# VectorE forms both halves of dt x B for the unit next to each activation table switch

## The chip, the cores and the metric

The kernel runs on one core of a Trainium2 chip. The metric is the device time of one launch in microseconds (us). The time before is the median of three runs.

## The reference

The input is a batch of 8 images of 192 channels with 56 x 56 positions, fp32. It goes through a stack of four layers: an involution (a 5 x 5 filter made from the input itself) and three selective-scan ("Mamba") layers. The scan is what matters here. For every position t of an image, every inner channel d and every one of 16 states n, each of the three layers computes

```
dt  = softplus(dbl[..., :rank] @ dt_proj.T + bias)      # dbl = xc @ x_proj.T
h   = exp(dt * A) * h + (dt * xc) * B                   # per d and n, over t
y   = sum over n of h * C   + xc * D
out = (y * silu(z)) @ out_proj.T                        # z and xc from in_proj; xc = silu(conv(...))
```

The first scan layer splits the 192 channels into three slices of 64 that share weights, each with 512 inner channels, and wraps them in layer norms. The second and third have 384 inner channels.

## The kernel before

**Tiling.** Each image is cut into 7 chunks of T = 448 positions, so there are 56 chunks. A job is one chunk of one scan: layer 1 has three jobs per chunk (168, one for each slice; i = 0, 1, 2 names the slice), layers 2 and 3 have one (56 each). The inner channels form nd groups of 128 (index j; nd = 4 in layer 1, 3 in layers 2 and 3), and the 16 states form four quarters (index q). A unit is one (job, j, q): its tile `uhg` has 128 partitions, which are 32 channels by 4 states, and 4 rows (NR) of T + 1 columns, so it covers 128 channels by 4 states. A job has nd x 4 units: 16 in layer 1, 12 in the others.

**The work of one unit k.** The rows of `uhg` are treated in two halves, h = 0 (rows 0 and 1) and h = 1 (rows 2 and 3).

- `inputs_begin` (L729, ScalarE) puts the carried state into column 0.
- `inputs_lo` (L738, VectorE) writes (dt x) B into half 0. The factor dt x is in the replica tile `reps[...][0]` in SBUF; the factor B comes from a PSUM bank, `brow`, which `spread_b` (L715, PE) fills with one matmul. The pool of this bank has one buffer, so the matmul for the next unit has to wait until the product has read the bank.
- `inputs_hi` (L734, GpSimd, called POOL below) writes (dt x) B into half 1, from `reps[...][1]` and from a copy of the same B row in SBUF, `rows[0, q]`, which a DMA brought.
- `decays` (L721, ScalarE) writes exp(dt A) into a PSUM tile for each half.
- `scan` (L742, VectorE) does the recurrence in place, one instruction for each half.
- `keep` (L746, ScalarE) copies the last column out as the carried state.
- `readout` (L751, POOL) multiplies the states by C in place, one instruction for each half.
- `reduce` (L757, L760, PE) adds the states up into `y`, and `gated` (L776, VectorE) applies silu(z).

The replica tiles are loaded by DMAs on SyncE's queue (L706, `load_ops`, two buffers) from the products dt and dt x of the job, which are stored to HBM. There are nine buffers for `uhg`.

**The loop.** `ssm_layer` issues the whole layer from one loop over the units. Each engine runs its instructions in the order of issue, and the code writes that order out by hand (`tc.manual_schedule()`), so there is no planner between the source and the queues. In iteration k come, in this order: reduction of unit k - 3, scan of half 0 of k, decays of half 0 of k + 1, `inputs_begin(k + 3)`, `inputs_hi(k + 2)`, readouts of k - 2, `inputs_lo(k + 1)`, `spread_b(k + 2)`, scan of half 1 of k, `keep(k)`, decays of half 1 of k + 1. Each iteration has two places (before the first scan, and before the second) where steps of the neighbouring jobs are run from a plan: the projections of the job to come, and the output projection of the job that has just ended (matmuls L1032 and L1034 in layer 1; L1107 in layers 2 and 3, with the addition L1113 on VectorE). `bounds` gives the places at which the stretches of the plan begin, and `places` spreads the steps over them.

**The table switches.** ScalarE's exponential and its silu and softplus need different activation tables. Once per job, a first block loads the silu table, does two activations (L587 for the coming job's xc, L568 for the running job's gate) and loads the table of the exponential again (L560). A second block does the same for the softplus (L634). `bounds` puts the first block at place `at[1]`, which is 6 in layer 1 (10 if the coming job is a slice 0) and 8 in the other layers, and the second at `at[3]`, 8 places later in layer 1 and 6 in the others. A place p belongs to iteration p // 2 of the job, so the product of that iteration on VectorE is that of unit p // 2 + 1 of the job. While a block runs, ScalarE makes no decays. Behind the first block come the matmul L592 with its copy L596 on ScalarE; behind the second come the products dt x (L641, VectorE), which read a matmul's result (L638).

**Filler.** `nothing` (L766, PE) issues matmuls with a zero weight into `y`; they do no computation.

Of the kernel before, what the change touches and what calls it, by code (L numbers as in the profile page):

```python
# [81 lines left out]
def conv_mamba_stack(ctx: ExitStack, tc: tile.TileContext, a, out):  # L82
    nc = tc.nc
# [478 lines left out]
    def with_gates(ops, u):  # L562


        def all_ops():
            ops()
            if u is not None:
                nc.scalar.activation(u.zs, u.zs, AF.Silu)  # L568

        table_block(all_ops)  # L570
# [113 lines left out]
    def ssm_layer(pool, w, jobs, n_slots):  # L684
# [10 lines left out]
        reps, brow, uhg, ys = {}, {}, {}, {}  # L695
# [15 lines left out]
        def spread_b(k):  # L711

            i, j, q = units[k]
            brow[k] = banks.b.tile([128, 512], F32, tag="b", name="b")
            nc.tensor.matmul(brow[k][:, :T], lhsT=pick_b[:, q, :], rhs=us[i].parts, start=True, stop=True)  # L715

        def decays(k, h):
            i, j, q = units[k]
            t = banks.da[h]
            for r in range(2):  # L720
                nc.scalar.activation(  # L721
                    t[:, 64 + 449 * r : 512 + 449 * r], reps[k // NQ][h][:, r, 0, :], AF.Exp, scale=w.neg_a[:, j * NR + 2 * h + r, q : q + 1]
                )

        def inputs_begin(k):
            i, j, q = units[k]
            uhg[k] = pool.tile([128, NR, T + 1], F32, tag="uhg", name="uhg", bufs=9)
            before = zeros[:, :NR] if jobs[i][1] else carry[jobs[i][0]][:, j, q, :]
            nc.scalar.copy(uhg[k][:, :, 0:1], before.unsqueeze(2))  # L729

        def inputs_hi(k):
            i, j, q = units[k]
            b = us[i].rows[0, q].unsqueeze(1).to_broadcast([128, 2, T])
            nc.gpsimd.tensor_mul(uhg[k][:, 2:4, 1:], reps[k // NQ][1][:, :, 1, :], b)  # L734

        def inputs_lo(k):
            b = brow[k][:, :T].unsqueeze(1).to_broadcast([128, 2, T])
            nc.vector.tensor_mul(uhg[k][:, 0:2, 1:], reps[k // NQ][0][:, :, 1, :], b)  # L738

        def scan(k, h):  # L740
            v = uhg[k][:, 2 * h : 2 * h + 2, :].rearrange("p r t -> p (r t)")
            nc.vector.tensor_tensor_scan(v, banks.da[h][:, 63:961], v, 0.0, ALU.mult, ALU.add)  # L742

        def keep(k):
            i, j, q = units[k]
            nc.scalar.copy(carry[jobs[i][0]][:, j, q, :].unsqueeze(2), uhg[k][:, :, T:])  # L746

        def readout(k, h):
            i, j, q = units[k]
            v = uhg[k][:, 2 * h : 2 * h + 2, 1:]  # L750
            nc.gpsimd.tensor_mul(v, v, us[i].rows[1, q].unsqueeze(1).to_broadcast([128, 2, T]))  # L751

        def reduce(k):
            i, j, q = units[k]
            if q == 0:
                ys[k // NQ] = banks.y.tile([128, 512], F32, tag="y", name="y")
                nc.tensor.matmul(ys[k // NQ][:, :T], lhsT=w.dd[:, j, :], rhs=us[i].xc[:, j, :], start=True, stop=False)  # L757
            y = ys[k // NQ]
            for r in range(NR):
                nc.tensor.matmul(y[32 * r : 32 * r + 32, :T], lhsT=fold, rhs=uhg[k][:, r, 1:], start=False, stop=(q == NQ - 1))  # L760

        def nothing(k, n):

            if k >= 0 and units[k][2] < NQ - 1:
                for _ in range(n):
                    nc.tensor.matmul(  # L766
                        ys[k // NQ][:, : nd * 112], lhsT=zeros, rhs=w.dd.rearrange("p j e -> p (j e)")[:, : nd * 112],
                        start=False, stop=False,
                    )

        def load_of(steps):
            return sum(st.cost for st in steps if st.matmuls)

        def gated(g):
            i, j = groups[g]
            nc.vector.tensor_mul(us[i].zs[:, j, :], us[i].zs[:, j, :], ys[g][:, :T])  # L776

        n_places = 2 * per_job
        def bounds(job):

            silu = 8 if nd == 3 else 10 if job[0] == 0 else 6
            softplus = silu + (6 if nd == 3 else 8)
            return 0, silu, silu + 2, softplus, softplus + 1, softplus + 4, n_places

        def places(*stretches):

            plan = [[] for _ in range(n_places)]
            for steps, first, end in stretches:  # L790
                todo, debt = list(steps), 0.0
                for p in range(first, end):
                    room, closed = (sum(st.cost for st in todo) + debt) / (end - p) - debt, False
                    while todo and (room > 1e-6 and not closed or p == end - 1):
                        if (todo[0].block if p % 2 else todo[0].settles) and p < end - 1:
                            break
                        plan[p].append(todo[0])
                        closed = todo[0].closes
                        room -= todo.pop(0).cost
                    debt = max(0.0, -room)  # L800
            return plan
# [11 lines left out]
        for k in range(3):  # L813
            inputs_begin(k)
        inputs_lo(0)
        spread_b(1)
        inputs_hi(0)
        inputs_hi(1)
        decays(0, 0)
        decays(0, 1)  # L820
# [3 lines left out]
        def load_when_free(k):  # L824

            g = len(reps)
            if g < len(groups) and k >= NQ * g - NQ - 1 and groups[g][1] in us[groups[g][0]].ops:
                load_ops(g)

        for k, (i, j, q) in enumerate(units):  # L830
            m = k % per_job
            if m == 0:

                fetch, outs, rest = tail
                if i + 1 < len(jobs):
                    u = us[i + 1]
                    at = bounds(jobs[i + 1])
                    plan = places(*zip((*jobs[i + 1][2](u, us[i], outs), rest + jobs[i + 1][3](u)), at, at[1:]))
                else:
                    gates = Step(None, lambda: with_gates(lambda: None, us[i]), 0, 0.3, block=True)  # L840
                    plan = places(([gates], 4, 6), (outs + rest, 8, n_places))
                plan[3][:0] = [Step(None, fetch, 2, 0.0)]

            if i + 1 < len(jobs) and m >= per_job - NQ:
                us[i + 1].row_in(0, m - (per_job - NQ))
            if i and m < NQ:
                us[i].row_in(1, m)
            if k >= NQ + 3 and q == 3:
                gated(k // NQ - 1)
            if k >= 3:  # L850
                reduce(k - 3)

            more = 3 - math.ceil(load_of(plan[2 * m] + plan[2 * m + 1]))
            nothing(k - 3, more > 2)
            bg.run(plan[2 * m])
            nothing(k - 3, more > 0)
            load_when_free(k)
            scan(k, 0)
            if k + 1 < n_units:
                decays(k + 1, 0)  # L860
            if k + 3 < n_units:
                inputs_begin(k + 3)
            if k + 2 < n_units:
                inputs_hi(k + 2)
            if k >= 2:
                readout(k - 2, 0)
                readout(k - 2, 1)
            if k + 1 < n_units:
                inputs_lo(k + 1)
            if k + 2 < n_units:  # L870
                spread_b(k + 2)
            bg.run(plan[2 * m + 1])
            nothing(k - 3, more > 1)
            load_when_free(k)
            scan(k, 1)
            keep(k)
            if k + 1 < n_units:
                decays(k + 1, 1)
            if m == per_job - 1:
                tail = jobs[i][4](us[i])  # L880
# [249 lines left out]
    for layer, w in enumerate((w1, w2, w3), 1):  # L1130
        with ExitStack() as stack:
            scan_banks(stack)
            pool = stack.enter_context(tc.tile_pool(name=f"ssm{layer}", bufs=1))
            load_weights(pool, w)
            with tc.manual_schedule():
                if layer == 1:
                    ssm_layer(pool, w, mamba_jobs(pool, w), 3)
                else:
                    ssm_layer(pool, w, dense_jobs(pool, w, layer), 1)
# [69 lines left out]
```

## Time and profile before

| What | Value |
|---|---|
| Median of three runs | 26491.58 us (26490.21 to 26491.7) |
| The profiled execution | 26518.46 us, its span 26516.6 us, mean PE clock 0.835 |
| PE, busy | 22170.8 us, 84% |
| VectorE (DVE), busy | 22849.2 us, 86% |
| ScalarE (ACT), busy | 17021.6 us, 64% |
| GpSimd (POOL), busy | 24242.3 us, 91% |
| Layer 1's scan | from 1658 to 18108 us |
| Layer 2's scan | from 18210 to 22363 us |
| Layer 3's scan | from 22434 to 26507 us |

The profile is of one execution on the chip. Its page gives busy times by engine, and groups of instructions, one for each line, engine and shape: a group has its count, its busy time, the mean duration of one in nanoseconds, and the idle time of the engine ahead of these instructions with what ended most of it. A line of the list of waits reads: who waited, for whom, the sum in us, the number of times, and the longest. In the timeline, each line is a start in us, a duration, the engine, the line, the operation with its operands, and, in brackets, idle time before it. An engine's busy share is not by itself a bound: an engine that is nearly always busy can still be one that nobody waits for. PEld is the load of weights on PE, which overlaps matmuls. The clock column is the granted PE clock as a share of full speed.

### The profile page before, as it was taken

How to read it: one execution, taken by the hardware profiler on the slowest of the kernel's cores; microseconds unless marked ns; L12 is line 12 of the kernel's file. 1: busy time of each engine (PE TensorE's matmuls, PEld its weight loads, DVE VectorE, ACT ScalarE, POOL GpSimd, SP SyncE). 2: the span in 40 equal slices, each digit the busy share in tenths (PEclk: the TensorE clock that was granted, in tenths of full speed). 3: DMA queues.
4: the chain of work that ended last, by engine and by line, in shares of the span. 5: the costliest groups of instructions: out<-in, count | busy, mean ns of one | idle time of the engine just before them, and what ended most of it. 6: DMA issues, size and time to landing. Idle time of an engine off the chain costs nothing. (4 is left out here: it accounts for less than half of the span.)

```text
span 26516.6 us, 248987 instructions
## 1 busy us (share of the span) xinstructions
PE 22170.8 (84%) x74628; PEld 7074.0 (27%) x74628; DVE 22849.2 (86%) x17677; ACT 17021.6 (64%) x32354; POOL 24242.3 (91%) x12820
## 2 busy tenths in 40 slices
PE   9988888888888888888878888888888888888888
PEld 3322222222222222222222222222333332333332
DVE  8878888888888888888888888887888887888888
ACT  1146666666666666666666666665666666777776
POOL 4469999999999999999999999998999998999999
PEclk9987878887778787787778877878888888888888
DMA  4433333333333333333333333333344443444443
GB/s 107 110 103 121 119 118 121 119 120 120 119 118 120 120 119 118 120 121 120 117 121 118 121 116 122 119 119 107 131 134 133 134 134 120 134 134 136 140 136 123
DMA packets 1249495, 3236.48 MB, mean 122 GB/s; under 512 B 170924, under 2 KB 510916, under 8 KB 1248008
## 3 DMA queue, kind: packets, MB, share of 16 engines
q1 hardware_dynamic: 1245336, 3219.49, 37.1%
q8 instruction: 585, 9.58, 0.1%
q14 instruction: 774, 6.34, 0.1%
q10 hardware_dynamic: 2800, 1.06, 0.0%
HBM read 2502.68 MB, written 555.55 MB: 115 GB/s over the span
## 5 line engine op out<-in xcount | busy, mean ns | idle before, releaser
L742 DVE TENSOR_TENSOR_SCAN uhg<-da,uhg 128x898 f32<-128x898 f32 x8064 | 16063.3, 2013 | 1003.2 <-ACT da L721 991.9
L751 POOL TENSOR_TENSOR uhg<-uhg,rows 128x896 f32<-128x896 f32 x8064 | 15387.2, 1930 | 809.0 <-ACT carry L746 769.7
L721 ACT ACTIVATE da<-rep,k 128x448 f32<-128x448 f32 x16128 | 10262.0, 636 | 1843.9 <-DVE uhg L742 1531.9
L734 POOL TENSOR_TENSOR uhg<-rep,rows 128x896 f32<-128x896 f32 x4032 | 8407.6, 2085 | 592.2 <-DMA rep<-ops 554.0
L738 DVE TENSOR_TENSOR uhg<-rep,b 128x896 f32<-128x896 f32 x4032 | 4296.4, 1066 | 923.9 <-PE b L715 873.4
L760 PE MATMUL y<-uhg,k 128*32 128x448 f32 x32256 | 4946.3, 658 | 124.0 <-POOL uhg L751 120.6
L746 ACT COPY carry<-uhg 128x4 f32<-128x4 f32 x4032 | 787.6, 195 | 4268.1 <-DVE uhg L742 4259.3
L715 PE MATMUL b<-k,k 96*128 96x448 bf16 x4032 | 1603.6, 398 | 1903.1 <-DVE uhg L738 1895.9
L766 PE MATMUL y<-w_d,k 128*128 128x448 f32 (+1 forms) x5908 | 3015.2, 608 | 0.0
L757 PE MATMUL y<-xc,w_d 128*128 128x448 f32 x2016 | 1411.4, 793 | 835.8 <-DVE zs L776 833.5
L1008 PE MATMUL mm<-xs,k 128*128 128x448 f32 x2688 | 1345.1, 628 | 571.4 <-ACT da L721 413.1
L766 PEld LDWEIGHTS y<-w_d,k 128*128 128x128 f32 x5908 | 1174.3, 220 | 1867.8 <-issue 1841.5
L626 PE MATMUL mm<-dbl,w_dt 36*128 36x448 f32 (+1 forms) x2016 | 1580.7, 897 | 36.1 <-ACT k L608 35.5
L760 PEld LDWEIGHTS y<-uhg,k 128*32 128x32 f32 x32256 | 749.9, 116 | 3182.6 <-issue 1554.8
L1060 PE MATMUL mm<-v,w_in 96*128 96x448 f32 x2688 | 1416.4, 658 | 152.0 <-ACT zs L668 97.7
L431 POOL TENSOR_TENSOR x<-x,one 96x448 f32<-96x448 f32 x560 | 633.2, 1135 | 648.8 <-DVE one L423 631.3
L641 DVE TENSOR_TENSOR dt<-dt,mm 128x448 f32<-128x448 f32 x1008 | 609.1, 618 | 644.5 <-PE mm L638 469.5
L715 PEld LDWEIGHTS <-k 96*128 96x128 bf16 x4032 | 414.7, 103 | 2741.1 <-issue 1641.0
L631 ACT ACTIVATE dt<-mm,k 128x448 f32<-128x448 f32 x1008 | 637.2, 632 | 771.8 <-PE mm L626 761.2
L423 DVE TENSOR_TENSOR prod<-mm,shifted 128x448 f32<-128x448 f32 x1680 | 932.3, 609 | 188.1 <-PE mm L411 167.6
L1087 PE MATMUL mm<-xin,w_conv 128*128 128x448 f32 x2688 | 1076.1, 543 | 0.0
L603 PE MATMUL mm<-dbl,k 16*16 16x448 f32 x1120 | 735.1, 747 | 273.6 <-ACT dbl L596 273.6
(134 smaller groups left out, 20183.0 us busy)
## 6 DMA issues: line engine op xcount, KB each, us to landing
rep<-ops SPq DMA_DIRECT2D x4032, 448.0 KB, 4.7
rows<-bc SPq DMA_DIRECT2D x2240, 224.0 KB, 4.9
ops<-dt SPq DMA_DIRECT2D x1008, 448.0 KB, 2.8
shifted<-xpad SPq DMA_DIRECT2D x672, 179.0 KB, 4.6
xg<-stream SPq DMA_DIRECT2D x168, 336.0 KB, 3.5
xr<-stream SPq DMA_DIRECT2D x168, 336.0 KB, 4.7
stream<-xr SPq DMA_DIRECT2D x112, 336.0 KB, 3.2
xs<-xg SPq DMA_DIRECT2D x224, 112.0 KB, 2.3
```

Source lines behind the costliest of these rows:

```text
L626: nc.tensor.matmul(u.dps[j][:, :T], lhsT=w.dtw[:, j * 128 : (j + 1) * 128], rhs=u.dbl[:nk, :], start=True, stop=True)
L715: nc.tensor.matmul(brow[k][:, :T], lhsT=pick_b[:, q, :], rhs=us[i].parts, start=True, stop=True)
L721: nc.scalar.activation(t[:, 64 + 449 * r : 512 + 449 * r], reps[k // NQ][h][:, r, 0, :], AF.Exp, scale=w.neg_a[:, j * NR + 2 * h + r, q : ...
L734: nc.gpsimd.tensor_mul(uhg[k][:, 2:4, 1:], reps[k // NQ][1][:, :, 1, :], b)
L738: nc.vector.tensor_mul(uhg[k][:, 0:2, 1:], reps[k // NQ][0][:, :, 1, :], b)
L742: nc.vector.tensor_tensor_scan(v, banks.da[h][:, 63:961], v, 0.0, ALU.mult, ALU.add)
L751: nc.gpsimd.tensor_mul(v, v, us[i].rows[1, q].unsqueeze(1).to_broadcast([128, 2, T]))
L757: nc.tensor.matmul(ys[k // NQ][:, :T], lhsT=w.dd[:, j, :], rhs=us[i].xc[:, j, :], start=True, stop=False)
L760: nc.tensor.matmul(y[32 * r : 32 * r + 32, :T], lhsT=fold, rhs=uhg[k][:, r, 1:], start=False, stop=(q == NQ - 1))
L766: nc.tensor.matmul(ys[k // NQ][:, : nd * 112], lhsT=zeros, rhs=w.dd.rearrange("p j e -> p (j e)")[:, : nd * 112], start=False, stop=False,)
L1008: nc.tensor.matmul(pm[:, :T], lhsT=w.inconv[:, k, j * 128 : (j + 1) * 128], rhs=ck.xs[:, i, 2 - 2 * k : 2 - 2 * k + T], start=(k == 0), st ...
L1060: nc.tensor.matmul(pm[:, :T], lhsT=w.inw[:, k, m * 128 : (m + 1) * 128], rhs=ck.v[:, k, :], start=(k == 0), stop=(k == NCT - 1),)
```

## The change

A set, `by_vector`, holds units for which VectorE makes both halves of (dt x) B. At the start of each job that has a successor, two units are put in: the one whose product VectorE makes in the iteration of the first block, and the same for the second block. For these units `inputs_hi` issues nothing, and `inputs_lo` issues two products in a row, half 0 and half 1, both with B from the PSUM bank.

```diff
+        by_vector = set()
+
         def inputs_hi(k):
+            if k in by_vector:
+                return
             i, j, q = units[k]
             b = us[i].rows[0, q].unsqueeze(1).to_broadcast([128, 2, T])
             nc.gpsimd.tensor_mul(uhg[k][:, 2:4, 1:], reps[k // NQ][1][:, :, 1, :], b)

         def inputs_lo(k):
             b = brow[k][:, :T].unsqueeze(1).to_broadcast([128, 2, T])
-            nc.vector.tensor_mul(uhg[k][:, 0:2, 1:], reps[k // NQ][0][:, :, 1, :], b)
+            for h in range(2 if k in by_vector else 1):
+                nc.vector.tensor_mul(uhg[k][:, 2 * h : 2 * h + 2, 1:], reps[k // NQ][h][:, :, 1, :], b)
...
                 if i + 1 < len(jobs):
                     u = us[i + 1]
                     at = bounds(jobs[i + 1])
+                    by_vector |= {k + at[1] // 2 + 1, k + at[3] // 2 + 1}
```

In layer 1 these are units 4 and 8 of a job, or 6 and 10 where the coming job is a slice 0; in layers 2 and 3 they are units 5 and 8. There are 167 + 55 + 55 = 277 jobs with a successor, so 554 of the 4032 units are concerned.

## The prediction

> **What bounds the kernel now.** I read the busy line of the page first, then the groups, the list of waits, the busy time by layer, and last the timeline around a table switch.
>
> ```profile
> PE 22170.8 (84%) x74628; PEld 7074.0 (27%) x74628; DVE 22849.2 (86%) x17677; ACT 17021.6 (64%) x32354; POOL 24242.3 (91%) x12820
> ...
> L742 DVE TENSOR_TENSOR_SCAN uhg<-da,uhg 128x898 f32<-128x898 f32 x8064 | 16063.3, 2013 | 1003.2 <-ACT da L721 991.9
> L751 POOL TENSOR_TENSOR uhg<-uhg,rows 128x896 f32<-128x896 f32 x8064 | 15387.2, 1930 | 809.0 <-ACT carry L746 769.7
> ...
> L734 POOL TENSOR_TENSOR uhg<-rep,rows 128x896 f32<-128x896 f32 x4032 | 8407.6, 2085 | 592.2 <-DMA rep<-ops 554.0
> L738 DVE TENSOR_TENSOR uhg<-rep,b 128x896 f32<-128x896 f32 x4032 | 4296.4, 1066 | 923.9 <-PE b L715 873.4
> ```
>
> POOL is the busiest engine, and the change takes work from it. Per unit it spends 2.085 + 2 x 1.930 = 5.9 us, VectorE 1.066 + 2 x 2.013 = 5.1 us. By layer (columns: stretch; length; busy PE, PEld, DVE, ACT, POOL; clock; DMA share; GB/s), layer 1 and then layer 2:
>
> ```profile
> 1658.30:18108.00 16449.70, 13294.60 (x42067) 3964.95 (x42066) 14285.63 (x9895) 11027.44 (x20959) 15653.56 (x8078) 0.80 0.35 119
> 18210.00:22363.00 4153.00, 3595.03 (x11953) 1252.18 (x11954) 3621.21 (x2621) 2875.43 (x5467) 3911.55 (x2023) 0.87 0.40 131
> ```
>
> POOL fills 95% and 94% of these stretches. But who waits for it?
>
> ```profile
> PE b L715 <- DVE uhg L738: 1895.9, 952, 11.4
> ...
> DVE uhg L742 <- ACT da L721: 991.9, 820, 3.9
> ...
> DVE uhg L738 <- PE b L715: 873.4, 707, 3.8
> ...
> POOL uhg L751 <- ACT carry L746: 769.7, 657, 3.3
> POOL uhg L734 <- DMA rep<-ops: 554.0, 106, 73.1
> DVE xr L1113 <- PE mm L1107: 362.6, 112, 3.6
> PE y L760 <- POOL uhg L751: 120.6, 173, 1.2
> DVE uhg L742 <- POOL uhg L751: 4.6, 10, 0.5
> ```
>
> Almost nobody: matmuls 120.6 us, VectorE 4.6 us plus 1.0 us behind L734, of 26,516.6. (Weight loads wait longer for POOL, 1122.8 us at L760, but under matmuls that still run: those show only the 120.6.) POOL is the one that waits, for the state that VectorE finishes and ScalarE copies out (L746). Following real gaps backwards in samples of each layer I find no POOL work on layer 1's chain and some 0 to 14% in layers 2 and 3, always just behind the replica DMA at a job's first units, never a product that the change removes. The loop runs VectorE, ScalarE, PE, and back.
>
> Now a switch, layer 2's first block. VectorE, then PE:
>
> ```profile
> 19639.39 1.09 DVE L738 TENSOR_TENSOR uhg<-rep,b 128x896 f32<-128x896 f32 x1
> 19643.55 0.62 DVE L1113 TENSOR_TENSOR xr<-xr,mm 96x448 f32<-96x448 f32 x1 [3.07 <-PE mm L1107]
> 19644.08 3.94 DVE L742 TENSOR_TENSOR_SCAN uhg<-da,uhg 128x898 f32<-128x898 f32 x2
> ```
>
> ```profile
> 19640.89 0.36 PE L715 MATMUL b<-k,k 96*128 96x448 bf16 x1
> 19641.09 4.67 PE L1107 MATMUL mm<-zs,w_out 128*96 128x448 f32 x12
> ```
>
> VectorE idles 3.07 us, so a second product has room. But its idling ends with PE's L1107, which stands behind the matmul that spreads B for the next unit (L715), and that one waits for VectorE to leave the only B bank.
>
> **What the skill says.** "GPSIMD Engine Reference", its introduction: ordinary elementwise work is roughly twice as fast on the Vector engine. The trace agrees: 2085 / 1066 = 1.96. The same page, section 1, has GpSimd and VectorE contend for SBUF only in a 2-port mode or with two SBUF inputs; the new product has one input in PSUM, as L738 has, so I add nothing for it. "TensorE: Matmul & The Clock Gate", Part 1, "What's actually happening", gives half clock after an idle window of about 3.4 us, windows running freely. The trace agrees: the granted clock here is 1.0 or 0.5, and its changes lie on a grid of 3.413 us.
>
> **The change part by part.** 277 switches have a next job (167 in layer 1, 55 in each other layer), with two units each: 554.
>
> Removed: 554 products on POOL, 554 x 2.085 = 1155 us. On the path: 0, cover being that nobody waits for them. Without that cover the most it can give back is what is waited for POOL, 120.6 + 5.6 = 126 us; POOL's own wait for the state grows in its place.
>
> Added: 554 products on VectorE, 1.066 us long, 0.98 from start to start (19642.0 would be the end of the second here): 541 us. At the first block the idle time behind it is 3.1 to 3.9 us in every layer (3.33 in layer 1's job at 10,003 us, where ScalarE's block of two table loads and two activations holds da back; 3.07 above). At the softplus block it is 0.46 before the unit's second scan plus 1.5 to 2.1 before L641, and in jobs ahead of a first layer-1 job 0.92 + 0.07 + 0.28. So VectorE itself pays nothing, or a few hundredths. Uncovered, all 541.
>
> Moved: L715 for the next unit, later by the second product less the time it already came after the first. Above: 19639.39 + 1.09 = 19640.48, and L715 started at 19640.89, 0.41 later; the delay is 0.98 - 0.41 = 0.57. Medians over the jobs, first block: 0.62 (running job first of three in layer 1), 0.95 (second), 0.97 (third), 0.50 (layer 2), 0.20 (layer 3, where PE is 0.89 behind anyway). At the softplus block L715 comes 1.8 to 3.6 us after the product: no delay.
>
> Where it lands: PE is in order, so what stands behind L715 is late too. Layers 2 and 3: L1107, then the addition L1113, the next scan, all of VectorE: paid in full, 55 x 0.50 = 27 and 55 x 0.20 = 11 us. Layer 1: behind L715 come L1032, L1034, a reduction and L592, whose result ScalarE copies (L596) only when its block and the decays are through; that copy comes 1.76 us after L592 (mean, first job of three, a quarter of them with none left), 3.05 and 3.65 us (second, third). So 56 x 0.17 = 10, 56 x 0.01 and 0 us.
>
> The new wait, of the second product for its half of the replica, is none: POOL read that half two units ahead. POOL's readouts move up by one product; SP's replica loads wait for the last unit of a group (L706), and the units concerned are never that, so no DMA moves by this edit.
>
> Sum: 27 + 11 + 10 = 48 us. The profiled execution, 26518.5 with 1.9 us outside its span, becomes 26,566; it stands 27 us over the median of the runs, so the median becomes 26,540 (+0.18%). What a measurement of this kernel can tell from no change is about 0.2%, 53 us, so this lies just inside.
>
> The unknown is PE's clock. Up to 1 us of idle time ahead of L715 may tip a window. In layer 1's third jobs the stretch behind the first block is cold in 27 of 55, and a cold one is 4.9 us longer (102.95 against 98.06); in layer 2, 22 of 53, 1.4 us each. At worst all go cold, 28 x 4.9 + 31 x 1.4 = +180; at best all go warm, 27 x 4.9 + 22 x 1.4 = -163. Jobs are partly locked to the windows, so a shift can move many together; nothing says which way, and I take zero.
>
> **The rivals.** *POOL is the bound (faster).* For it: 94 to 95% busy, the fullest rows of the page. Against: the waits. It gives at most 126 us back: 26,366, or 26,414 with the 48 us paid. All 1155 us (25,336) would need VectorE, with 541 us more to do, to lose most of its waits for ScalarE and PE too. It decides where more than about 100 us of waiting for POOL goes.
>
> *The clock turns warm (faster).* For it: half of the third jobs are warm as it is. Against: more idle time before a burst is no help by itself. 26,540 - 163 = 26,377 at best; it outweighs the delay by 0.2% from 21 third jobs fewer cold, (48 + 53) / 4.9.
>
> *The clock turns cold (slower).* 14 to 28 third jobs more cold, 69 to 137 us: 26,609 to 26,677, with layer 2 up to 26,720. For it: PE's idle time grows exactly where the windows are near the edge.
>
> *VectorE pays.* If the scans wait for the products at both blocks, 26,491 + 541 = 27,032; at the softplus block alone, half. Against: the gaps above.
>
> That the change does nothing it says is excluded: POOL loses exactly 554 products in the order of instructions, nothing else moves.
>
> **How the numbers follow.** Delay of L715 with the clock about as before: 0.50, 26,540, its own range 26,510 to 26,575, half of it under the 0.2% mark. Cold: 0.22. Warm: 0.13, of which 0.03 within the mark. POOL: 0.10. VectorE pays: 0.05. Faster 0.10 + 0.10 = 0.20; same 0.25 + 0.03 = 0.28; slower 0.25 + 0.22 + 0.05 = 0.52. The range leaves out VectorE's case and the outer half of warm and cold: 26,410 to 26,690.
>
> **What would show it.** Right: POOL's product at 3478 instead of 4032 and VectorE's at 4586; POOL's wait for L746 up from 770 towards 1,900 us; VectorE's waits for da, L638 and L1107 together down by nearly 500; L715's wait for L738 up by some 180; jobs of layer 2 longer by 0.5 us than 74.1, of layer 3 by 0.2 than 72.7, layer 1's 97.9 the same. Wrong: layer 1 shorter with PE's wait for POOL gone (POOL), a clock in layer 1 away from 0.80 with the time (clock), scans that follow the second product without a gap at a block (VectorE).

## The result and the profile after

The changed kernel takes 26,349.13 us (median of five runs, 26,329.46 to 26,383.98) against 26,490.21 us of the kernel before in the same comparison: a ratio of 0.9956 (95% interval 0.9942 to 0.9971; ratios here are close to those of the means, which lie 116 us apart, where the medians lie 141 us apart). It is 116 to 141 us faster where I had forecast 50 us slower. The profiled execution took the median itself, 26,349.13 us, and its span is 26,347.3 us, 169 us shorter than the one shown of before, which was a slow one for its kernel: 27 us above its median.

Seven lines that the change adds shift the later line numbers: L734 is now L739, L738 is L744, L742 is L748, L746 is L752, L751 is L757, L760 is L766, L1034 is L1041, L1107 is L1114. The busy line and the groups of the page after:

```profile
PE 22116.2 (84%) x74628; PEld 7068.1 (27%) x74628; DVE 23362.5 (89%) x18231; ACT 17020.7 (65%) x32354; POOL 23132.2 (88%) x12266
...
L748 DVE TENSOR_TENSOR_SCAN uhg<-da,uhg 128x898 f32<-128x898 f32 x8064 | 16060.1, 2013 | 676.7 <-ACT da L721 672.5
L757 POOL TENSOR_TENSOR uhg<-uhg,rows 128x896 f32<-128x896 f32 x8064 | 15366.2, 1929 | 1374.4 <-ACT carry L752 1317.2
...
L739 POOL TENSOR_TENSOR uhg<-rep,rows 128x896 f32<-128x896 f32 x3478 | 7247.3, 2084 | 967.1 <-DMA rep<-ops 864.0
L744 DVE TENSOR_TENSOR uhg<-rep,b 128x896 f32<-128x896 f32 x4586 | 4846.6, 1067 | 856.8 <-PE b L715 805.7
```

POOL has 1110 us less to do and VectorE 513 us more, as the counts said (3478 and 4586 products). The time that POOL gained went into its own waits. From the list of waits:

```profile
PE b L715 <- DVE uhg L744: 2067.2, 1102, 12.1
...
POOL uhg L757 <- ACT carry L752: 1317.2, 1109, 4.9
...
POOL uhg L739 <- DMA rep<-ops: 864.0, 100, 72.9
...
DVE uhg L748 <- ACT da L721: 672.5, 556, 2.9
...
DVE xr L1120 <- PE mm L1114: 301.0, 112, 2.7
...
DVE dt L641 <- PE mm L638: 194.8, 218, 2.2
```

PE's L715 waits 171 us longer for VectorE, as forecast (180). But VectorE's waits fell too: for the decays from 991.9 to 672.5, for L638 from 469.5 to 194.8, for the output projection of layers 2 and 3 from 362.6 to 301.0. That is 656 us less, more than the 541 us of products put into them; L641's waits for the second block itself (L634, 107.0 to 175.0) and for nothing that shows (40.3 to 100.2) take 128 us of it back.

Where the time went, from the start of each job's first scan to the next one's, summed over the jobs:

| jobs | before | after | difference |
|---|---|---|---|
| layer 1, slice 0 (56 jobs) | 5550.2 us | 5514.8 us | -35 us |
| layer 1, slice 1 (56) | 5279.5 us | 5187.6 us | -92 us |
| layer 1, slice 2 (55) | 5525.2 us | 5423.3 us | -102 us |
| layer 2 (55) | 4078.7 us | 4126.8 us | +48 us |
| layer 3 (55) | 3998.0 us | 4012.4 us | +14 us |

These sums are of one execution each. In two runs below that have no second product at the first block, the slices come to 5532 to 5548, 5228 to 5247 and 5510 to 5527 us, so up to some 50 us of slice 1's difference can lie between executions; layer 2, in five runs that leave it as it was, comes to 4058 to 4082 us.

Layers 2 and 3 pay for the delay of L715 as I had worked out, somewhat more than the 38 us. Layer 1, where I had put +10 us, gains 229 us in this pair of executions (a run with the change in layer 1 alone, below, puts it at 174). So the question is layer 1.

PE's timeline of one job of slice 1 shows what moves (the same job in both, from its fourth unit). Before, with the busy times and, third from the right, the clock of two parts of its last stretch:

```profile
7646.71 0.35 PE L715 MATMUL b<-k,k 96*128 96x448 bf16 x1 [1.01 <-DVE uhg L738]
...
7647.88 3.22 PE L1034 MATMUL mm<-zs,w_out 128*64 128x448 f32 x8
...
7651.92 3.20 PE L592 MATMUL mm<-xc,w_x 128*36 128x448 f32 x8
...
7658.81 0.92 PE L603 MATMUL mm<-dbl,k 16*16 16x448 f32 x2 [2.51 <-ACT dbl L596]
...
7662.76 1.67 PE L603 MATMUL mm<-dbl,k 16*16 16x448 f32 x2
...
7666.33 3.35 PE L626 MATMUL mm<-dbl,w_dt 36*128 36x448 f32 x4
```

```profile
7658.80:7661.26 2.46, 2.45 (x7) 0.75 (x8) 2.46 (x2) 2.38 (x6) 2.46 (x2) 1.00 0.09 23
7661.27:7669.70 8.43, 8.43 (x18) 1.97 (x19) 7.77 (x6) 4.88 (x10) 8.35 (x5) 0.50 0.20 62
```

After:

```profile
7560.41 0.56 PE L715 MATMUL b<-k,k 96*128 96x448 bf16 x1 [2.01 <-DVE uhg L744]
...
7562.57 5.47 PE L1041 MATMUL mm<-zs,w_out 128*64 128x448 f32 x8
...
7568.86 3.20 PE L592 MATMUL mm<-xc,w_x 128*36 128x448 f32 x8
...
7573.18 0.92 PE L603 MATMUL mm<-dbl,k 16*16 16x448 f32 x2
...
7576.40 0.92 PE L603 MATMUL mm<-dbl,k 16*16 16x448 f32 x2
...
7579.13 3.35 PE L626 MATMUL mm<-dbl,w_dt 36*128 36x448 f32 x4
```

```profile
7573.10:7577.37 4.27, 4.27 (x18) 1.10 (x18) 4.27 (x4) 3.82 (x9) 4.15 (x3) 1.00 0.05 13
7577.39:7582.50 5.11, 5.11 (x14) 1.46 (x10) 5.11 (x4) 2.89 (x6) 4.51 (x3) 0.50 0.31 106
```

L715 waits 2.01 us instead of 1.01, by the second product. Within that idle time, at 7560.31 us, the clock falls to half, and the output projection takes 5.47 us instead of 3.22. But it has slack. What follows it, the reduction and L592, is pushed against L603, and the 2.51 us of idle time ahead of L603 are gone. PE now works in the 3.4 us ahead of L603, and the clock falls only 4.2 us after L603 has begun, where it fell after 2.45 us before: the second pair of L603 takes 0.92 us instead of 1.67, while the last four L626 take 3.35 us as before. That second stretch is the one that counts: L603, L604 and L626 make the dt of the coming job, and the second block, its products L641 and the scans behind them wait for it. In slices 1 and 2 of before, the end of the last L626 and the length of the job go together (correlation 0.99).

This job itself gains nothing, 93.51 us before and 93.61 after: it gets to L603 1.7 us later, which uses up what the clock gives. The gain shows over all jobs.

Over all jobs of layer 1 but the very first, with means of times from the start of the scan at which the first block falls:

| running slice | first to last L603, before | after | their clock under 0.75, before | after |
|---|---|---|---|---|
| 0 | 15.42 to 21.22 us | 16.03 to 20.67 us | 58% of jobs | 0% |
| 1 | 15.17 to 21.62 us | 15.68 to 20.14 us | 98% | 18% |
| 2 | 16.59 to 22.31 us | 16.12 to 20.65 us | 42% | 4% |

The stretch ends 0.6 to 1.7 us earlier, although in two of the three slices it starts later. That is the gain: per job it is 0.6, 1.6 and 1.9 us by slice. PE's idle time between the end of L592 and L603 fell from 1.38, 2.45 and 2.49 us on the mean to 0.09, 0.27 and 1.53.

Two further counts say how. In slices 1 and 2 of before, the clock was at half when L603 began in 19 of 56 and in 23 of 55 jobs; these took 95.0 and 103.7 us, the others 93.9 and 98.1. After, no job of these slices begins so. The long jobs of slice 2 account for its 102 us: 23 x 5.6 = 130, less 0.5 us that the other 32, and now all, take longer. And the kernel before has in slice 0 what the change brings about: in 23 of 56 jobs the output projection already ran below the full clock, and all of these had no idle time ahead of L603 and a stretch above 0.75; the other 33 had at least 2.06 us, and all were below it. Slice 2 is different: its output projection is warm (at the full clock, where cold is half) in every job, before and after, and its idle time of before was 2.49 us in short and long jobs alike. So idle time alone did not decide there, and that the 1.0 us less of it is what ends the long jobs is not shown.

### The profile page after: what moved, and what is told of

It reads as the page before. It is cut to its first block, busy times and chain, and to the rows that moved or that the text cites. A ratio compares the mean times of both kernels' runs of the same rounds, so it can differ in the third digit from the quotient of the medians.

```text
span 26347.3 us, 248997 instructions
## 1 busy us (share of the span) xinstructions
PE 22116.2 (84%) x74628; PEld 7068.1 (27%) x74628; DVE 23362.5 (89%) x18231; ACT 17020.7 (65%) x32354; POOL 23132.2 (88%) x12266
## 5 line engine op out<-in xcount | busy, mean ns | idle before, releaser
L748 DVE TENSOR_TENSOR_SCAN uhg<-da,uhg 128x898 f32<-128x898 f32 x8064 | 16060.1, 2013 | 676.7 <-ACT da L721 672.5
L757 POOL TENSOR_TENSOR uhg<-uhg,rows 128x896 f32<-128x896 f32 x8064 | 15366.2, 1929 | 1374.4 <-ACT carry L752 1317.2
L739 POOL TENSOR_TENSOR uhg<-rep,rows 128x896 f32<-128x896 f32 x3478 | 7247.3, 2084 | 967.1 <-DMA rep<-ops 864.0
L744 DVE TENSOR_TENSOR uhg<-rep,b 128x896 f32<-128x896 f32 x4586 | 4846.6, 1067 | 856.8 <-PE b L715 805.7
L766 PE MATMUL y<-uhg,k 128*32 128x448 f32 x32256 | 4937.7, 663 | 123.4 <-POOL uhg L757 121.1
L752 ACT COPY carry<-uhg 128x4 f32<-128x4 f32 x4032 | 787.4, 195 | 4235.4 <-DVE uhg L748 4233.9
L715 PE MATMUL b<-k,k 96*128 96x448 bf16 x4032 | 1608.7, 399 | 2069.5 <-DVE uhg L744 2067.2
L766 PEld LDWEIGHTS y<-uhg,k 128*32 128x32 f32 x32256 | 740.5, 116 | 3149.7 <-issue 1696.5
L626 PE MATMUL mm<-dbl,w_dt 36*128 36x448 f32 (+1 forms) x2016 | 1451.3, 830 | 25.8 <-ACT k L608 25.3
L715 PEld LDWEIGHTS <-k 96*128 96x128 bf16 x4032 | 415.5, 103 | 3051.8 <-DVE uhg L744 1627.4
L641 DVE TENSOR_TENSOR dt<-dt,mm 128x448 f32<-128x448 f32 x1008 | 606.6, 617 | 498.3 <-PE mm L638 194.8
L1029 PE MATMUL mm<-xs,k 64*128 64x448 f32 x1344 | 907.1, 773 | 63.0 <-ACT zs L666 60.7
```

The lines of the kernel that those rows point to most:

```text
L626: nc.tensor.matmul(u.dps[j][:, :T], lhsT=w.dtw[:, j * 128 : (j + 1) * 128], rhs=u.dbl[:nk, :], start=True, stop=True)
L744: nc.vector.tensor_mul(uhg[k][:, 2 * h : 2 * h + 2, 1:], reps[k // NQ][h][:, :, 1, :], b)
```

## The experiments

Two theories. **Shift**: the longer hold of the B bank is what acts; it moves PE's slack work, and with it the clock windows. **GpSimd**: POOL was the bound after all, and its 1110 us are the cause. Each run stands beside runs of the kernel before on the same chip (medians 26,468 to 26,473 us), and its ratio is to those. In all short diffs, "+" and "-" are against the kernel before, where nothing else is said, and `by_vector` is filled as in the change. Sums by slice and layer are of one execution each, as above.

### GpSimd relieved, nothing added

```diff
         def readout(k, h):
+            if h == 1 and k + 4 in by_vector:
+                return
```

> GpSimd relieved, nothing added: both products stay where they were before, and in the iterations in which the change takes a product from GpSimd, its readout L751 of half 1 of the unit read out there is left out (554 x 1.93 us; these states are not multiplied by C, so the output is another one). Shift theory (the longer hold of the B bank moves PE's work and with it the clock): no change from before, 26,490 +- 50 us, layer 1's jobs 97.9 us on the mean as before. GpSimd theory (its queue was the bound): as fast as the change or faster, 26,350 us or less.

Measured: 26,420.39 us, ratio 0.9984 (0.9977 to 0.9990). POOL has 1014 us less to do than in the profile before, nearly the relief of the change, and some 42 to 53 us of a thousand come back (by the ratio and by the medians), more than the shift theory had allowed. Layer 1's jobs keep the pattern of before (98.79, 93.70 and 100.49 us by slice; before 99.11, 94.28, 100.46; after 98.48, 92.64, 98.61). The largest single part is layer 3, 3955.1 us instead of 3998.0 (3987 to 4004 in the five runs that leave this layer as it was). So POOL is not the bound of layer 1, but its relief was not worth quite nothing. Why not, a window of the kernel before shows, with PE's and then POOL's timeline:

```profile
24708.75 1.62 PE L760 MATMUL y<-uhg,k 128*32 128x448 f32 x8
24710.29 0.36 PE L715 MATMUL b<-k,k 96*128 96x448 bf16 x1
```

```profile
24705.54 3.82 POOL L751 TENSOR_TENSOR uhg<-uhg,rows 128x896 f32<-128x896 f32 x2
```

The eight records of a reduction (an fp32 matmul leaves two) take 0.96 us elsewhere at this clock, here 1.62: the second four wait for the second readout, which ends at 24,709.36, and start 0.05 us later. This wait lies inside a group and shows as no idle time. In layer 3 it holds back L715 at the first block; with the readout gone, that unit takes 8.65 us on the mean instead of 9.17.

### VectorE loaded, GpSimd not relieved

```diff
             nc.vector.tensor_mul(uhg[k][:, 0:2, 1:], reps[k // NQ][0][:, :, 1, :], b)
+            if k in by_vector:
+                spare = pool.tile([128, 2, T], F32, tag="spare", name="spare")
+                nc.vector.tensor_mul(spare, reps[k // NQ][1][:, :, 1, :], b)
```

> The reverse: GpSimd keeps all its products, and VectorE makes a second product from the B bank for the same 554 units, into a spare tile that nobody reads. Shift theory: as the change, 26,350 +- 40 us, with layer 1 about 230 us shorter and layers 2 and 3 about 60 us longer. GpSimd theory: slower than before by the delay, 26,540 us.

Measured: 26,366.28 us, ratio 0.9964 (0.9950 to 0.9978). The interval overlaps with that of the change, and the sums by slice and layer are its own within 11 us: 5514.7, 5187.5, 5424.1, 4115.8, 4017.6. Its busy line has POOL fuller than ever:

```profile
PE 22147.9 (84%) x74628; PEld 7078.3 (27%) x74628; DVE 23362.5 (89%) x18231; ACT 17027.5 (65%) x32354; POOL 24252.0 (92%) x12820
```

A product that nobody reads makes the kernel 0.36% faster. It takes VectorE's time and holds the bank: in the job of slice 1 shown above, L715 waits 2.01 us for it, as in the change. What VectorE's time does by itself, this run does not say.

### One block at a time

```diff
-                    by_vector |= {k + at[1] // 2 + 1, k + at[3] // 2 + 1}
+                    by_vector |= {k + at[1] // 2 + 1}
```

(against the kernel after; the other run keeps `at[3]`.)

> The change at the first block (silu) alone, 277 units. Shift theory: all of it is there, since only there the bank's matmul waits: 26,350 +- 40 us. GpSimd theory: half of the gain, about 26,420 us.

> The change at the second block (softplus) alone, 277 units. Shift theory: nothing, 26,490 +- 40 us, since the next spread matmul comes 1.8 to 3.6 us after the product anyway. GpSimd theory: half of the gain, about 26,420 us.

Measured: the first block alone 26,370.13 us, ratio 0.9966 (0.9953 to 0.9979), with layer 1 by slice at 5515.5, 5190.9 and 5420.0 us, as in the change. The second alone 26,463.23 us, ratio 0.9999 (0.9990 to 1.0007). Half of the moved products do nothing that shows, and it is the half at which L715 does not wait.

### Layer 1 alone

```diff
-                    by_vector |= {k + at[1] // 2 + 1, k + at[3] // 2 + 1}
+                    by_vector |= {k + at[1] // 2 + 1, k + at[3] // 2 + 1} if nd == 4 else set()
```

(against the kernel after.)

> The change in layer 1 alone (334 units). Shift theory: layer 1 as in the change, layers 2 and 3 as before, so faster than the change by their 62 us: 26,285 +- 40 us. GpSimd theory: a smaller gain than the change, since 220 units keep their GpSimd product: 26,400 us or more.

Measured: 26,297.46 us, ratio 0.9935 (0.9920 to 0.9950). Layers 2 and 3 are at 4057.7 and 4002.4 us: what the delay cost there is given back.

### B from the row in SBUF, the bank let go early

```diff
             for h in range(2 if k in by_vector else 1):
-                nc.vector.tensor_mul(uhg[k][:, 2 * h : 2 * h + 2, 1:], reps[k // NQ][h][:, :, 1, :], b)
+                nc.vector.tensor_mul(uhg[k][:, 2 * h : 2 * h + 2, 1:], reps[k // NQ][h][:, :, 1, :], row if h else b)
```

(against the kernel after; `row` is the row that `inputs_hi` used.)

> The change, but VectorE's second product takes B from the row in SBUF that GpSimd would have used, so the B bank is let go after the first product as before; VectorE's and GpSimd's counts are those of the change. Shift theory: the wait of the spread matmul is as before, so there is no gain in layer 1 and no loss in layer 2: 26,470 +- 50 us, down by up to 40 us where layer 3 profits from GpSimd being earlier. A theory by which VectorE's or GpSimd's own work is what counts: 26,350 us or less.

Measured: 27,196.58 us, ratio 1.0279 (1.0263 to 1.0294). Neither theory had this, and the run does not decide between them. The bank is let go early (in layer 1, L715 starts 0.05 us after the first product, in the median), yet the jobs of slice 1 take only 5100.6 us, while those of slice 0 take 5903.1. So a longer hold is not the only thing that moves them; with a VectorE that is late by several us, hold and lateness are not told apart here. Two groups of the list by shape show what was slow:

```profile
L746 DVE TENSOR_TENSOR uhg<-rep,b 128x896 f32<-128x896 f32 x4032 | 4287.0, 1063 | 710.2 <-PE b L715 657.3 <-DMA rep<-ops 39.8
L746 DVE TENSOR_TENSOR uhg<-rep,rows 128x896 f32<-128x896 f32 x554 | 2268.9, 4095 | 0.0
```

The same product with both inputs in SBUF takes 4.1 us on the mean, against 1.07 with B in PSUM. It took from 1.15 to 10.6 us, with a median of 2.2. "GPSIMD Engine Reference", section 1 ("Specifications"), has GpSimd and VectorE contend for SBUF in just this case, two SBUF inputs. The slow products fit that, but the trace does not prove it: POOL has instructions running for 87 to 91% of the time in those over 7 us, and for all of it in those under 1.5 us. The size, up to 9.5 us more than 1.07, is this run's.

### A filler instead of a delay

If PE's idle time ahead of L603 is the cause, then filling it should do as well as closing it. No product is moved here; four matmuls with zero weights (a form that the kernel has, L766; eight records) go ahead of L603 in layer 1, for coming jobs of slices 1 and 2.

```diff
-            [Step(xproj, xproj_out, 0, nd)] * (nd == 4) + [pause(1.0 if nd == 4 else 3.5)]
+            [Step(xproj, xproj_out, 0, nd)] * (nd == 4) + [pause(1.0 if nd == 4 else 3.5), Step(None, lambda: u.fill(), 9, 0.0)]
...
+            u.fill = lambda i=i: nothing(now[0] - 3, 4 if nd == 4 and i % 3 else 0)
```

> The kernel before, no product moved; in layer 1, for coming jobs of slice 1 and 2, four matmuls with zero weights (a form that the kernel has already, L766) are put into PE's idle time right ahead of L603. Shift theory, clock half: the stretch from L603 to L626 runs at the full clock, and the jobs of running slices 0 and 1 gain as in the change, 127 us together: 26,350 +- 50 us. If the clock is only an accompaniment: 26,470 us or more (the filler is extra work).

Measured: 26,368.55 us, ratio 0.9964 (0.9950 to 0.9978). The total is as expected, the split is not: the jobs of slice 1 gain 190 us against the execution shown of before (5089.5 us), but those of slice 0 lose 66 (5616.5 us), since there L603 now starts at 18.13 us instead of 15.42, behind the filler and a cold output projection. So the filler goes where the idle time is, with slice 1 running (`i % 3 == 2` for the coming job):

> The four filler matmuls as before, but only where the running job is a slice 1 (there 2.5 us of idle time stood ahead of L603; with the running slice 0 the filler made L603 later and the jobs longer). Shift theory: slice 1's jobs at 90.9 us instead of 94.3, 3.4 x 56 = 190 us: 26,285 +- 40 us.

Measured: 26,219.21 us, ratio 0.9905 (0.9890 to 0.9919), the fastest of all, and below the expected span. PE's timeline of the same job as above, from L592:

```profile
7557.19 3.20 PE L592 MATMUL mm<-xc,w_x 128*36 128x448 f32 x8
...
7561.50 3.27 PE L766 MATMUL y<-w_d,k 128*128 128x448 f32 x8
7564.71 0.92 PE L603 MATMUL mm<-dbl,k 16*16 16x448 f32 x2
...
7567.94 0.92 PE L603 MATMUL mm<-dbl,k 16*16 16x448 f32 x2
...
7569.83 1.77 PE L626 MATMUL mm<-dbl,w_dt 36*128 36x448 f32 x4
```

L603 begins 0.6 us later after L592 than before the edit, and yet the last four L626 take 1.77 us instead of the 3.35 of both kernels: the full clock holds to the end, as it does in 47 of the slice's 56 jobs and in none of before. The slice's jobs take 5044.8 us, 235 less than in the execution shown of before. Slices 0 and 2, which have no filler, gain 38 and 62 us as well, part of which can lie between executions. In slice 2 the clock is at half when L603 begins in 8 jobs instead of 23. Nothing was edited there, so it seems that a job's place against the clock's windows depends on the jobs ahead of it.

### Twice the hold, and both means together

Holding the bank for a further product at the first block, in layer 1 alone:

> First block of layer 1 alone, and the B bank is held for one product more still (into a spare tile that nobody reads), so the spread matmul comes 2 us later than before, where it came 1 us later in the change. Shift theory: the 1.5 to 2.5 us of idle time ahead of L603 are used up, so slices 0 and 1 lose again: 26,330 us (26,290 to 26,420), slower than the change in layer 1 alone by about 40 us. A theory by which a longer hold is better: under 26,270 us.

Measured: 26,414.13 us, ratio 0.9978 (0.9970 to 0.9987), at the far end of the expected span, and 117 us slower than one product in layer 1. The place was another than expected: slice 1 is no worse (5181.8 us); slice 2 goes back to 5516.0, where its output projection, warm in all jobs with one product, is now cold in 98% of them, and L603 starts at 17.69 us instead of 16.12; slice 0 is at 5555.2.

> What the runs so far point to: in layer 1 the change at the first block only, where the running job is a slice 0 or 2 (35 + 102 us), and the filler where it is a slice 1 (190 us); layers 2 and 3 as before. Shift theory: 26,475 - 327 = 26,150 +- 60 us, if the gains add; jobs are locked to the clock's windows, so they may add in part only: under 26,260 us in any case.

Measured: 26,240.26 us, ratio 0.9915 (0.9898 to 0.9932), within the stated limit but 90 us above the sum, and no faster than the filler alone (0.9905; the intervals overlap). With products held in slices 0 and 2, slice 1's jobs take 5150.6 us instead of 5044.8: the last L626 are cold again in 66% of them, against 16%. The gains do not add.

## Why the prediction was wrong

**The step that failed** is "nothing says which way, and I take zero", for PE's clock. It was not zero: layer 1, for which I had put +10 us, came out 174 us shorter with the change in layer 1 alone, and 229 us in the pair of executions shown. I had the mechanism as a rival (0.13, "the clock turns warm") and ruled against it with "more idle time before a burst is no help by itself". What the runs show in its place, for slices 0 and 1: the idle time ahead of L715 makes one stretch cold that has slack, and takes away idle time ahead of another that has none. The sum of idle time does not tell that; its place does. I had followed the delay only as far as L596 ("that copy comes 1.76 us after L592"), counted the slack there as cover, and not asked what PE does in that slack: it stood idle, just ahead of the critical stretch. That was readable as 2.51 us of wait ahead of L603, and the jobs of slice 0 of before had shown what its absence does. For slice 1 the filler shows by itself that the clock of this stretch pays; slice 2's gain is without a cold stretch ahead, and its cause stays open in part. That the hold of the bank is what moves PE, and not VectorE's lateness, rests on L715's wait in the timelines; the run that was to part the two did not.

**Its best case was too narrow.** "At best all go warm, 27 x 4.9 + 22 x 1.4" counted cold jobs of slice 2 and of layer 2. For slice 2 this came nearly true: 27 x 4.9 is 132 us, and it gained 102. The cold stretches of slices 0 and 1 (58% and 98% of their jobs) were not in it. So layer 1 gained more than the 132 us counted there.

**Right:** the counts; the cover on VectorE (the second block alone: ratio 0.9999); the delay of L715, 1.00 us in the job shown and 171 us of further wait in all (forecast 180); that it is paid in layers 2 and 3. The unit of L1107 takes 9.40 us instead of 8.83 in layer 2 and 9.42 instead of 9.17 in layer 3, so 0.57 and 0.25 us a job where 0.50 and 0.20 were forecast, 31 and 14 us. The rest of layer 2's 48 us lies in other units, or between executions. (One figure of the working is wrong, without effect on the sum: the second product of the example would end at about 19,641.5 us, not at 19,642.0.)

**Half right:** "On the path: 0" for POOL. Against layer 1 it holds: the relief alone leaves the pattern there, and PE's wait for POOL stayed (120.6 us before, 121.1 after). But the list of waits that it was read from leaves out waits inside a group of matmuls, and layer 3 had such a one. Relief alone is worth some 42 to 53 us (ratio 0.9984). In the change it is not to be seen: with and without it, the unit of L1107 in layer 3 takes 9.42 us, since L715 there starts within 0.1 us of the end of the second product.

**The sign to watch was a poor one.** I named "a clock in layer 1 away from 0.80". It stayed at 0.80 over the stretch of layer 1, and the mean clock of the execution fell from 0.835 to 0.832 although the kernel became faster: the mean does not tell cold stretches that count from those that don't.

## What to carry to other kernels

Where an engine's speed depends on its recent use, a delay or a piece of filler is judged by which stretch loses or gains idle time, not by how much there is: follow a delayed engine to its next idle gap, and see whether the work behind that gap is on the path. A mean clock hides this; durations of the same instruction by place show it. And when an edit that moves work turns out faster, run its two halves apart before giving the credit to the work that was moved: here the half with the dummy product had the whole gain, and a filler without any of it gave more.

## What was not expected of the hardware

- A VectorE product of 128 x 896 with both inputs in SBUF took 4.1 us on the mean (1.15 to 10.6) beside a busy GpSimd, against 1.07 us with one input in PSUM. GpSimd's readouts slowed only from 1.93 to 1.96 us, on the mean.
- The clock fell while PE was busy. In the job shown of before, PE is busy without a gap from 7658.81 us on, mostly with matmuls of 16 x 16 and 36 x 128 weights, and the clock falls at 7661.26, with 0.96 us of idle time in the 3.4 us ahead of the fall. In the job shown of after it falls at 7577.38, with no idle time of PE in the 3.4 us ahead. This is so in 156 of the 167 jobs of layer 1 with a successor, for the first fall behind the start of L603. "TensorE: Matmul & The Clock Gate", Part 1, speaks of idle windows of about 3.4 us; here the clock fell without one. These records suggest that small matmuls count for less than large ones; no run of its own shows it.
- Gains from the clock in neighbouring jobs did not add (26,240 us instead of 26,150), and jobs without an edit came out 100 us shorter (by one execution each) with an edit in the jobs ahead.
